# One pool for the tiles of products in a two-layer cross-attention kernel, the order of two weight loads, and the last visit's scaling

## The chip, the cores and the metric

The kernel runs on one core of a Trainium2 chip. Its engines are named as the profile names them: PE (TensorE; its weight loads are the row PEld), DVE (VectorE), ACT (ScalarE), POOL (GpSimd) and SP (SyncE, which here only issues DMAs). The metric is the device time of one execution in microseconds (us), as a median of several runs.

## The reference

Two cross-attention layers with 20 heads of 32 are applied to x (8 batches, 100 rows, 640 channels). Each context has 722 tokens of 1024 channels: 77 of text and 645 of "ip" tokens. Cut to what matters:

```python
q = split(x @ Wq);  k, v = split(text @ Wk), split(text @ Wv)
k_ip, v_ip = split(ip @ Wk_ip), split(ip @ Wv_ip)
out = attend(q, k, v) + attend(q, k_ip, v_ip)       # layer 1
x = merge(out) @ Wo + bo + x

# layer 2: the same with its own weights, and the ip part as
sem = (softmax(q @ k_text.T * scale) @ text) @ ip.T * scale
ip_probs = softmax(q_h @ k_ip.T * scale + 0.5 * sem) * spatial_mask
x = merge(attend(q, k, v) + ip_probs @ v_ip) @ Wout + bout + x
```

Everything is in fp32. The ip tokens' K and V products, 8 x 645 tokens by 1024 by 640 channels for each of four weight matrices, are most of the arithmetic.

## The kernel before, in words

The kernel has a first stage and a main stage.

**First stage (lines 257 to 473).** Inside a nested stack of pools it computes q of layer 1 and, for both layers, k and v of the text tokens and v of the few ip tokens left over after five blocks of 128. Its SBUF tiles come from a pool called "first", which is closed when the stage ends. The text products use a seven-product scheme (`seven`, L187): two-by-two blocked matrices multiplied with seven block products and some additions, where ACT copies a product out of PSUM into the result tile and DVE adds others to it. The result tiles `kt` (L341) and `vt` (L382) have the tag "evs" with two buffers in "first". When a block is finished, POOL issues DMAs that write it to DRAM (L356, L394).

**Main stage.** After "first" and its PSUM pool are closed, new pools are opened (L475 to L484): PSUM pools `ps_sc` for scores (two tags of two banks each, one buffer) and `ps_pt` (two buffers of one bank, for transposes, values and small products), and SBUF pools, the first of which is `opool`, called "made", with two buffers. Tiles in it are the results of the seven-product scheme for the ip tokens: `ko` (L674) for K, `vo` (L644) for V. Where a new pool lies on space that a closed pool held, the first user of a new tile waits for the users of the old ones.

For the first pair of batches and the first two blocks of tokens the task list begins (L714 to L722) with loads: `load_w4` (L550) loads the quarters of the K weights' fifth chunk of 128 channels, two into the tile `wk4` and two into tiles of the pools "tail" and "one"; `load_wv` loads the four quarters of V's ip weights. Then come seven K products (`psk`), the sums of V's weight quarters on DVE (`weight_sums`, L131), seven more K products, the fifth chunk's weight sums and its seven products, and then the V products (`psv`).

**Order.** PE, DVE and ACT run in the order in which the code records the instructions (L44, `manual_schedule`); what SP and POOL issue is placed by a scheduler.

**Visits.** Attention runs over `ORDER`, a list of (unit, chunk): 16 units (a layer and a batch) by 5 chunks of four heads, 80 visits. A visit computes scores in two parts (`scores`, L980), the softmax on DVE and ACT, and then the scaling of the exponentials: `factors` (small operations on DVE, the last L1041), `scaled` (ACT, four instructions of 100x512 at L1047), and `scaled_rest` (DVE, L1055 for the ip tokens after the first 512 and L1051 for text). These are put in the list `later` and recorded at later points. The next visit does `transposes` (L1076): six groups of four PE transposes, each group into a bank of `ps_pt` and copied from there by ACT or DVE (L1088, L1090), and `values` (L1092): 24 products, copied by DVE (L1110). In the last five visits the products' tasks run out. After the last visit the code at L1354 to L1360 records the rest: `last_out` (L950) for the previous visit's values, the six transposes with `at_end=True`, an addition to the residual and its store, `values`, the last `last_out`, its addition and store.

Of the kernel before, what the change touches and what calls it, by code (L numbers as in the profile page):

```python
# [9 lines left out]
F32 = mybir.dt.float32  # L10
AF = mybir.ActivationFunctionType
ALU = mybir.AluOpType
AX = mybir.AxisListType

P = 128
B = 8
S = 100
C = 640
# [5 lines left out]
KA = 512  # L24
# [9 lines left out]
HC = C // 2  # L34
# [6 lines left out]
ORDER = [(u, c) for u in range(NU - 2) for c in range(NC_)]  # L41
# [5 lines left out]
def two_layer_xattn(  # L47
# [17 lines left out]
    nc = tc.nc  # L65
# [3 lines left out]
    wpool = ctx.enter_context(tc.tile_pool(name="w", bufs=1))  # L69
    cpool = ctx.enter_context(tc.tile_pool(name="ctx", bufs=2))  # L70
    spool = ctx.enter_context(tc.tile_pool(name="sums", bufs=1))
    dram = ctx.enter_context(tc.tile_pool(name="scratch", bufs=1, space=bass.MemoryType.DRAM))


# [182 lines left out]
    with ExitStack() as es:  # L257
        fp = es.enter_context(tc.tile_pool(name="first", bufs=1))
# [29 lines left out]
        nc.sync.dma_start(mask_sb[:, 1:2], mask)  # L288


        zeros = fp.tile([P, 2 * S], F32, tag="zeros", name="zeros")
        nc.vector.memset(zeros, 0.0)
        ps = product_ps("zeros_ps")
        for _ in range(4):
# [34 lines left out]
        def text_k(l):  # L329
            t = fp.tile([P, 2, 512], F32, tag="ev", name=f"kt4_{l}", bufs=2)  # L330
            for h in range(2):
                ps = product_ps(f"pskt4_{l}_{h}")
                for k in range(NCC):
                    nc.tensor.matmul(
                        ps[:, :TH], lhsT=W["k", 4][:, k, :], rhs=text[:, k, TH * h : TH * (h + 1)],
                        start=(k == 0), stop=(k == NCC - 1),
                    )
                nc.scalar.copy(t[:, h, :TH], ps[:, :TH])
            nc.gpsimd.dma_start(kt_d[l][4].rearrange("p (h n) -> p h n", h=2), t[:, :, :TH])
            for r in range(2):  # L340
                t = fp.tile([P, 2, 2, C // 2], F32, tag="evs", name=f"kt_{l}_{r}", bufs=2)  # L341

                def product(ps, which, go_on, r=r):
                    for k in range(HK):
                        nc.tensor.matmul(
                            ps[:, :TH], lhsT=W["k", WHICH[which]][:, k, r * P : (r + 1) * P],
                            rhs=sums[which][:, k, :],
                            start=(k == 0 and not go_on), stop=(k == HK - 1), skip_group_check=True,
                        )

                for f in seven(
                    f"pskt_{l}_{r}", product, tuple(t[:, h, m, :TH] for h in range(2) for m in range(2))
                ):
                    f()
                for m in range(2):
                    nc.gpsimd.dma_start(  # L356
                        kt_d[l][2 * m + r].rearrange("p (h n) -> p h n", h=2), t[:, :, m, :TH]
                    )
# [20 lines left out]

        def text_v_blocks(l):  # L380
            for r in range(2):
                t = fp.tile([P, 2, 2, HC], F32, tag="evs", name=f"vt_{l}_{r}", bufs=2)  # L382

                def product(ps, which, go_on, r=r):
                    for k in range(HK):
                        nc.tensor.matmul(
                            ps[:, :HC], lhsT=sums[which][:, k, r * P : (r + 1) * P], rhs=W["v", WHICH[which]][:, k, :],
                            start=(k == 0 and not go_on), stop=(k == HK - 1), skip_group_check=True,
                        )

                for f in seven(f"psvt_{l}_{r}", product, tuple(t[:, h, m] for h in range(2) for m in range(2))):
                    f()
                for h in range(2):
                    nc.gpsimd.dma_start(  # L394
                        vt_d[l][h * TH + r * P : h * TH + (r + 1) * P, :].rearrange("r (m n) -> r m n", m=2), t[:, h]
                    )
# [78 lines left out]
    ps_sc = ctx.enter_context(tc.tile_pool(name="ps_sc", bufs=1, space=PSUM))  # L475
    ps_pt = ctx.enter_context(tc.tile_pool(name="ps_pt", bufs=2, space=PSUM))
    pj[0] = ps_pj
    opool = ctx.enter_context(tc.tile_pool(name="made", bufs=2))
    kpool = ctx.enter_context(tc.tile_pool(name="k", bufs=2))
    vpool = ctx.enter_context(tc.tile_pool(name="v", bufs=2))  # L480
    tpool = ctx.enter_context(tc.tile_pool(name="tail", bufs=2))
# [91 lines left out]
    def pair_tasks(us):  # L573
# [15 lines left out]
        for js in ((0, 1), (2, 3), (4,)):  # L589
# [113 lines left out]
            def with_sums(j, steps, fourth_sum=fourth_sum):  # L703

                return (
                    steps[:1] + [(0.0, lambda: third_sum(j))] + steps[1:4] + [(0.0, lambda: fourth_sum(j))] + steps[4:]
                )
# [6 lines left out]
            if first:  # L714

                v_load = (0.0, lambda: load_wv(wvi[0]))
                v_sums = (0.0, lambda: ([f() for f in weight_sums("v", HC)], load_text(us)))
                v = v_steps(0)
                ks_ = ks_[7:] + [(0.0, w4_sums)] + ks_[:7]
                tasks += [(0.0, load_w4), v_load] + with_sums(0, with_sums(1, ks_[:7]))  # L720
                tasks += [v_sums] + ks_[7:]
                tasks += v[:2] + [(0.0, text_sum)] + v[2:] + v_steps(1)  # L722
            else:

                if js[0]:
                    tasks[ahead:ahead] = head(js[0])
                else:
                    first_sums[us] = head(0)
                for j in js:
                    v = with_sums(j, v_steps(j))  # L730
                    if len(js) == 2 and j == js[0]:
                        v[-2:-2] = head(js[1])
                    tasks += v
                    marks[f"v {j}"] = len(tasks)
                    if j == NB - 1 and us[0] + 2 < B:
                        tasks.append((0.0, lambda: load_text([u + 2 for u in us])))
                tasks += ks_
# [242 lines left out]
    def scores(u, c, part):  # L980
# [31 lines left out]
        def exponentials(h):  # L1012
            for i in (2 * h, 2 * h + 1):
                dst = p[:, i, k0 : k0 + n]
                nc.scalar.activation(  # L1015
                    dst, dst if l else scs[h][:S, i % 2, :n], AF.Exp, bias=st[:, part, i : i + 1],
                    scale=-1.0 if l else 1.0, accum_out=st[:, 3 + part, i : i + 1],
                )
# [13 lines left out]
        def text_exponentials():  # L1032
            nc.scalar.activation(f, f, AF.Exp)
            nc.scalar.activation(p[:, :, NI:], p[:, :, NI:], AF.Exp)

        def factors():
            nc.vector.tensor_reduce(st[:, 5, :], p[:, :, NI:], AX.X, ALU.add)
            nc.vector.tensor_tensor(st[:, 3:5, :], st[:, 3:5, :], f, ALU.mult)
            nc.vector.tensor_tensor(st[:, 4, :], st[:, 3, :], st[:, 4, :], ALU.add)
            nc.vector.reciprocal(rz, st[:, 4:6, :])  # L1040
            nc.vector.scalar_tensor_tensor(  # L1041
                mul, f, mask_sb[:, l : l + 1], rz[:, 0:1, :].to_broadcast([S, 2, 4]), ALU.mult, ALU.mult
            )
# [5 lines left out]
        def scaled_rest(text):  # L1049
            if text:  # L1050
                nc.vector.tensor_tensor(  # L1051
                    p[:, :, NI:], p[:, :, NI:], rz[:, 1, :].unsqueeze(2).to_broadcast([S, 4, NT]), ALU.mult
                )
            else:
                nc.vector.tensor_tensor(  # L1055
                    p[:, :, KA:NI], p[:, :, KA:NI], mul[:, 1, :].unsqueeze(2).to_broadcast([S, 4, NI - KA]),
                    ALU.mult,
                )
# [3 lines left out]
        if part == 0:  # L1062
            later.append((True, lambda: exponentials(0)))
            later.append((True, lambda: exponentials(1)))
        else:
            for h in range(2):
                text_maxima(h)
            differences()
            later.append((True, lambda: (exponentials(0), exponentials(1), text_exponentials())))
            later.append((False, lambda: (factors(), scaled_rest(False))))  # L1070
            later.append((False, lambda: (scaled((0, 1)), scaled_rest(True))))
            later.append((False, lambda: scaled((2, 3))))
# [3 lines left out]
    def transposes(u, c, j, at_end=False):  # L1076
        if j == 0:
            emit(len(later))
            pts[u, c] = one.tile([P, 6, 4 * S], F32, tag="pt", name=f"pt_{u}_{c}")
        rows = P if j < 5 else NTAIL  # L1080
        ps = ps_pt.tile([P, 512], F32, tag="pt", name=f"pspt_{u}_{c}_{j}")
        for i in range(4):
            nc.tensor.transpose(  # L1083
                ps[:rows, i * S : (i + 1) * S], pr[u, c][:, i, j * P : j * P + rows], ident[:S, :S]
            )
        dst, src = pts[u, c][:rows, j, :], ps[:rows, : 4 * S]
        if j in (2, 4) or at_end and j == 0:
            nc.scalar.copy(dst, src)  # L1088
        else:
            nc.vector.tensor_copy(dst, src)  # L1090
# [316 lines left out]
```

## Time and profile before

| What | us |
|---|---|
| Median of 3 runs (2051.62 to 2052.35) | 2052.03 |
| The profiled execution's own time | 2052.75 |
| Its span, from the first to the last instruction | 2051.0 |
| PE busy in it | 2027.9 |
| DVE busy | 1129.7 |
| ACT busy | 784.5 |
| POOL busy | 275.1 |

A table of longer stretches shows where PE is not busy:

```profile
0.00:200.00 200.00, 198.50 (x1027) 146.54 (x1028) 53.38 (x70) 20.75 (x49) 21.96 (x42) 1.00 0.61 193
200.00:230.00 30.00, 24.19 (x94) 19.39 (x92) 10.25 (x14) 1.12 (x3) 4.87 (x7) 0.89 0.55 161
230.00:2030.00 1800.00, 1791.23 (x13845) 1393.73 (x13846) 1054.89 (x2928) 752.82 (x2169) 248.28 (x384) 1.00 0.40 116
2030.00:2051.00 21.00, 13.96 (x199) 11.78 (x198) 11.14 (x36) 9.77 (x28) 0.00 (x0) 0.99 0.07 25
```

Its columns are the stretch in us from the span's start, its length, the busy time of PE, PEld, DVE, ACT and POOL with the number of their instructions, the TensorE clock granted as a share of the full one, the mean busy share of the DMA engines, and GB/s. A matmul that waits is not busy; one that runs at a lower clock is, so idle time and lost clock are read from different columns. The first stage ends, and the main stage begins, at about 203 us.

### The profile page before, as it was taken

How to read it: one execution, taken by the hardware profiler on the slowest of the kernel's cores; microseconds unless marked ns; L12 is line 12 of the kernel's file. 1: busy time of each engine (PE TensorE's matmuls, PEld its weight loads, DVE VectorE, ACT ScalarE, POOL GpSimd, SP SyncE). 2: the span in 40 equal slices, each digit the busy share in tenths (PEclk: the TensorE clock that was granted, in tenths of full speed). 3: DMA queues.
4: the chain of work that ended last, by engine and by line, in shares of the span. 5: the costliest groups of instructions: out<-in, count | busy, mean ns of one | idle time of the engine just before them, and what ended most of it. 6: DMA issues, size and time to landing. Idle time of an engine off the chain costs nothing.

```text
span 2051.0 us, 38714 instructions
## 1 busy us (share of the span) xinstructions
PE 2027.9 (99%) x15162; PEld 1571.4 (77%) x15162; DVE 1129.7 (55%) x3046; ACT 784.5 (38%) x2247; POOL 275.1 (13%) x433
## 2 busy tenths in 40 slices
PE   9999899999999999999999999999999999999998
PEld 9676767776876867778678777777777778889876
DVE  2223322245555455554557665655665667778787
ACT  1001000043334243333433344444544455566676
POOL 0101212110120111111111001001010101111110
PEclk9999999999999999999999999999999999999999
DMA  9544222313342434325346354336342536545461
GB/s 341 152 136 149 89 85 83 102 60 97 100 115 72 138 119 112 91 76 152 97 127 168 93 168 119 86 96 188 95 118 80 148 99 169 151 132 154 119 187 54
DMA packets 296484, 252.20 MB, mean 123 GB/s; under 512 B 46638, under 2 KB 265442, under 8 KB 296302
## 3 DMA queue, kind: packets, MB, share of 16 engines
q1 hardware_dynamic: 274254, 181.19, 32.4%
q0 software_dynamic: 21776, 68.44, 9.3%
q8 instruction: 119, 1.95, 0.4%
q14 instruction: 63, 0.52, 0.1%
q10 hardware_dynamic: 272, 0.10, 0.0%
HBM read 180.74 MB, written 68.93 MB: 122 GB/s over the span
## 4 chain that ended last, share of the span: by engine, by line
PE 95%; DVE 3%; ACT 1%; issue 1%; DMA 0%; ACTq 0%; DVEq 0%
PE psv_a L637 9%; PE psv_d L637 8%; PE pspt L1083 8%; PE psk_a L667 8%; PE psk_d L667 8%; PE sc L992 6%; PE pv L1106 4%; PE psv_e L637 4%; PE psk_c L667 4%; PE psv_b L637 4%; PE psv_c L637 4%; PE psk_e L667 4%; PE psk_b L667 4%; PE pso L904 3%; PE psq L304 2%; PE psq L923 2%
## 5 line engine op out<-in xcount | busy, mean ns | idle before, releaser
L1015 ACT ACTIVATE p<-sc,st 100x512 f32<-100x512 f32 (+1 forms) x320 | 165.6, 529 | 201.9 <-DVE st L1001 120.4
L1047 ACT ACTIVATE p<-p,st 100x512 f32<-100x512 f32 x320 | 208.0, 713 | 51.3 <-DVE st L1041 51.1
L1083 PEld LDWEIGHTS pspt<-ident,p 100*128 100x128 f32 (+1 forms) x1920 | 187.1, 137 | 44.3 <-issue 5.5
L1090 DVE COPY pt<-pspt 128x400 f32<-128x400 f32 (+1 forms) x319 | 175.4, 569 | 81.7 <-PE pspt L1083 73.3
L1083 PE MATMUL pspt<-ident,p 100*128 100x100 f32 (+1 forms) x1920 | 210.0, 250 | 7.3 <-DVE pt L1090 2.1
L1015 ACT ACTIVATE p<-p,st 100x512 f32<-100x512 f32 (+1 forms) x320 | 176.6, 554 | 77.9 <-DVE st L1007 77.8
L637 PE MATMUL psv_a<-wv,x 128*128 128x397 f32 (+1 forms) x560 | 185.8, 474 | 0.6 <-DVE ko L227 0.3
L1088 ACT COPY pt<-pspt 128x400 f32<-128x400 f32 x161 | 79.1, 491 | 264.0 <-PE pspt L1083 263.5
L637 PE MATMUL psv_d<-wv,s 128*128 128x320 f32 (+1 forms) x560 | 174.4, 454 | 0.0
L691 POOL DMA_DIRECT2D k_d<-ko x140 | 100.3, 720 | 460.8 <-DVE ko L227 407.3
L637 PEld LDWEIGHTS psv_a<-wv,x 128*128 128x128 f32 x560 | 103.0, 189 | 68.7 <-issue 13.3
L1007 DVE CUSTOM_DVE_ANT_0 p<-sc,sem 100x512 f32<-100x512 f32 (+1 forms) x320 | 138.7, 490 | 21.8 <-PE sc L992 20.9
L637 PEld LDWEIGHTS psv_d<-wv,s 128*128 128x128 f32 x560 | 103.6, 190 | 52.0 <-issue 2.5
L667 PE MATMUL psk_a<-x,wk 128*128 128x256 f32 (+1 forms) x672 | 137.1, 349 | 4.6 <-ACT ko L201 4.6
L1001 DVE TENSOR_REDUCE st<-sc 100x2 f32<-100x1024 f32 (+1 forms) x160 | 125.3, 825 | 28.7 <-PE sc L992 28.7
L992 PE MATMUL sc<-k,q 32*100 32x210 f32 (+1 forms) x1280 | 138.5, 502 | 0.0
L667 PE MATMUL psk_d<-s,wk 128*128 128x256 f32 (+1 forms) x672 | 136.6, 348 | 0.0
L667 PEld LDWEIGHTS psk_a<-x,wk 128*128 128x128 f32 x672 | 110.5, 190 | 22.9 <-ACT ko L201 5.0
L667 PEld LDWEIGHTS psk_d<-s,wk 128*128 128x128 f32 x672 | 108.5, 189 | 20.4 <-issue 6.7
L652 POOL DMA_DIRECT2D v_d<-vo x70 | 38.9, 556 | 624.6 <-DVE gst L627 318.6
L637 PE MATMUL psv_e<-wvt,x 128*128 128x397 f32 (+1 forms) x280 | 92.9, 474 | 0.0
L1106 PEld LDWEIGHTS pv<-pt,v 128*32 128x32 f32 x3200 | 67.5, 110 | 26.1 <-issue 16.3
(217 smaller groups left out, 3305.4 us busy)
## 6 DMA issues: line engine op xcount, KB each, us to landing
x<-ip_t SPq DMA_DIRECT2D x80, 512.0 KB
k<-k_d SPq DMA_DIRECT2D x80, 322.5 KB
v<-v_d SPq DMA_DIRECT2D x80, 320.0 KB
v_d<-vo POOLq DMA_DIRECT2D x70, 320.0 KB, 2.5
k_d<-ko POOLq DMA_DIRECT2D x112, 128.0 KB, 4.1
o<-wo SPq DMA_DIRECT2D x35, 320.0 KB
x<-ip_t SPq DMA_DIRECT2D x20, 532.0 KB
q<-wq SPq DMA_DIRECT2D x20, 320.0 KB
```

Source lines behind the costliest of these rows:

```text
L637: nc.tensor.matmul(ps[:, :m], lhsT=tokens(k)[:, :P], rhs=w[:, k, :], start=(k == 0 and not go_on), stop=(k == HK - 1), skip_group_check=True,)
L667: nc.tensor.matmul(ps[:, i * m : (i + 1) * m], lhsT=w[:, k, :], rhs=tokens(k), start=(i == 0 and k == 0 and not go_on), stop=(k == HK - 1) ...
L691: nc.gpsimd.dma_start(dst[:, :, r], src)
L992: nc.tensor.matmul(scs[i // 2][:S, i % 2, : k1 - k0], lhsT=qs_[u][rows, c, :], rhs=ks[u, c][rows, k0:k1], start=True, stop=True)
L1001: nc.vector.tensor_reduce(st[:, part, 2 * h : 2 * h + 2], scs[h][:S, :, :n], AX.X, ALU.max, negate=True)
L1007: nc.vector.tensor_tensor_reduce(out=p[:, i, k0 : k0 + n], in0=scs[h][:S, i % 2, :n], in1=sems[u][:, k0 : k0 + n], scale=-1.0, scalar=3.0e ...
L1015: nc.scalar.activation(dst, dst if l else scs[h][:S, i % 2, :n], AF.Exp, bias=st[:, part, i : i + 1], scale=-1.0 if l else 1.0, accum_out= ...
L1047: nc.scalar.activation(p[:, i, :KA], p[:, i, :KA], AF.Copy, scale=mul[:, 0, i : i + 1])
L1083: nc.tensor.transpose(ps[:rows, i * S : (i + 1) * S], pr[u, c][:, i, j * P : j * P + rows], ident[:S, :S])
L1088: nc.scalar.copy(dst, src)
L1090: nc.vector.tensor_copy(dst, src)
L1106: nc.tensor.matmul(ps[32 * i : 32 * i + 32, :S], lhsT=lhs, rhs=pt[:rows, j, i * S : (i + 1) * S], start=(j == 0), stop=(j == 5),)
```

## The change

The pool "made" is opened before the first stage, and the text stage's `kt` and `vt` blocks are tiles of it; the tag "evs" in "first" is gone, and a tile of zeros shares the tag of another small tile. `load_w4` and `load_wv` change places in the first pair's list of tasks. In the last visit the scaling is recorded in one piece: ACT scales heads 0 and 1, and a DVE multiplication with a broadcast operand scales heads 2 and 3 of the first 512 tokens, ahead of the two `scaled_rest` operations. The last visit's transposes 2 and 3 go to the PSUM banks of the scores in place of those of `ps_pt`.

```diff
@@ -69,6 +69,7 @@
     cpool = ctx.enter_context(tc.tile_pool(name="ctx", bufs=2))
     spool = ctx.enter_context(tc.tile_pool(name="sums", bufs=1))
+    opool = ctx.enter_context(tc.tile_pool(name="made", bufs=2))
     dram = ctx.enter_context(tc.tile_pool(name="scratch", bufs=1, space=bass.MemoryType.DRAM))
@@ -288,7 +289,7 @@
-        zeros = fp.tile([P, 2 * S], F32, tag="zeros", name="zeros")
+        zeros = fp.tile([P, 2 * S], F32, tag="evl", name="zeros")
@@ -338,7 +339,7 @@
             for r in range(2):
-                t = fp.tile([P, 2, 2, C // 2], F32, tag="evs", name=f"kt_{l}_{r}", bufs=2)
+                t = opool.tile([P, 2, 2, C // 2], F32, tag="made", name=f"kt_{l}_{r}")
@@ -379,7 +380,7 @@
             for r in range(2):
-                t = fp.tile([P, 2, 2, HC], F32, tag="evs", name=f"vt_{l}_{r}", bufs=2)
+                t = opool.tile([P, 2, 2, HC], F32, tag="made", name=f"vt_{l}_{r}")
@@ -475,7 +476,6 @@
     pj[0] = ps_pj
-    opool = ctx.enter_context(tc.tile_pool(name="made", bufs=2))
     kpool = ctx.enter_context(tc.tile_pool(name="k", bufs=2))
@@ -717,7 +717,7 @@
                 ks_ = ks_[7:] + [(0.0, w4_sums)] + ks_[:7]
-                tasks += [(0.0, load_w4), v_load] + with_sums(0, with_sums(1, ks_[:7]))
+                tasks += [v_load, (0.0, load_w4)] + with_sums(0, with_sums(1, ks_[:7]))
@@ -1067,6 +1067,16 @@
             later.append((True, lambda: (exponentials(0), exponentials(1), text_exponentials())))
+            if (u, c) == ORDER[-1]:
+
+                later.append((False, lambda: (
+                    factors(), scaled((0, 1)),
+                    nc.vector.tensor_tensor(
+                        p[:, 2:, :KA], p[:, 2:, :KA], mul[:, 0, 2:].unsqueeze(2).to_broadcast([S, 2, KA]), ALU.mult
+                    ),
+                    scaled_rest(False), scaled_rest(True),
+                )))
+                return
             later.append((False, lambda: (factors(), scaled_rest(False))))
@@ -1078,7 +1088,10 @@
         rows = P if j < 5 else NTAIL
-        ps = ps_pt.tile([P, 512], F32, tag="pt", name=f"pspt_{u}_{c}_{j}")
+        if at_end and j in (2, 3):
+            ps = ps_sc.tile([P, 2, 512], F32, tag=f"sc{j - 2}", name=f"pspt_{u}_{c}_{j}")[:, 0]
+        else:
+            ps = ps_pt.tile([P, 512], F32, tag="pt", name=f"pspt_{u}_{c}_{j}")
         for i in range(4):
```

## The prediction

> **What bounds the kernel now.** I read the page first, then the table by stretches of time, then the list of waits, then the chain of waits in the two places where the table shows TensorE (PE) short of work. The page says that PE is the bound nearly everywhere:
>
> ```profile
> span 2051.0 us, 38714 instructions
> PE 2027.9 (99%) x15162; PEld 1571.4 (77%) x15162; DVE 1129.7 (55%) x3046; ACT 784.5 (38%) x2247; POOL 275.1 (13%) x433
> PE 95%; DVE 3%; ACT 1%; issue 1%; DMA 0%; ACTq 0%; DVEq 0%
> ```
>
> PE is idle for only 2051.0 - 2027.9 = 23.1 us, so a change that adds or removes no matmul can be worth at most about that, plus what a lowered clock costs. Stretches of 10 us show two places with idle PE: 200 to 230 us, where the text stage hands over to the first K products, and the last 15 us. In steps of 2 us the first place looks like this (columns: stretch, its length, busy PE, PEld, DVE, ACT, POOL, granted PE clock, DMA share, GB/s):
>
> ```profile
> 204.00:206.00 2.00, 2.00 (x11) 1.74 (x10) 0.20 (x1) 0.00 (x0) 1.26 (x2) 1.00 0.89 239
> 206.00:208.00 2.00, 1.13 (x6) 0.64 (x4) 0.00 (x0) 0.00 (x0) 0.14 (x1) 1.00 0.97 294
> 208.00:210.00 2.00, 0.00 (x0) 0.00 (x0) 0.00 (x0) 0.00 (x0) 0.00 (x0) 1.00 0.33 129
> 210.00:212.00 2.00, 0.31 (x1) 0.32 (x2) 0.33 (x1) 0.37 (x1) 0.00 (x0) 0.72 0.02 6
> 212.00:214.00 2.00, 2.00 (x6) 1.55 (x6) 0.69 (x2) 0.00 (x0) 0.00 (x0) 0.50 0.94 274
> 214.00:216.00 2.00, 2.00 (x6) 1.64 (x5) 0.00 (x0) 0.37 (x1) 0.00 (x0) 0.50 0.84 218
> 216.00:218.00 2.00, 2.00 (x7) 1.58 (x7) 0.00 (x0) 0.00 (x0) 0.00 (x0) 0.57 0.99 264
> 218.00:220.00 2.00, 2.00 (x11) 1.75 (x10) 1.02 (x2) 0.00 (x0) 0.00 (x0) 1.00 0.73 232
> ```
>
> The reader should see two losses: no PE work from 207.1 to 211.7, and then about 6 us in which PE is "busy" at half clock, with 6 matmuls in 2 us where it later does 11. The list of waits names the first:
>
> ```profile
> ACT ko L201 <- DMA vt_d<-vt: 15.7, 1, 15.7
> PE psk_a L667 <- ACT ko L201: 4.6, 1, 4.6
> ```
>
> and the chain of waits orders it:
>
> ```profile
> 204.73 5.93 DMA vt_d<-vt
> ...
> 211.26 0.38 ACT ko L201
> 211.64 0.04 issue
> 211.69 3.78 PE psk_a L667 x8
> 215.47 2.90 PE psk_c L667 x8
> ```
>
> PE finished the first two of the seven products, but ACT could not empty the first: its target `ko` is the first tile of the pool "made" (L478), laid where the closed pool "first" was. So it waited for all users of that space, the last being the write of `vt` to DRAM, issued at 204.73.
>
> [...] 4.56 us idle, then 0.50. [...] the `vt` writes here land after 3.0 us in the median and 5.93 us for the last one, beside the weight loads. [...]
>
> **Part 1, one pool for made tiles.** The pool is now opened before "first", and the text stage's `kt`/`vt` blocks are its earlier tiles. The first `ko` thus takes over the buffer of the last-but-one `vt` block, with two writes of its own to wait for (issued at 187.26 and 189.67, long landed). The waits in the changed program say the same: the first ACT copy of `ko` holds only two DMA counts and PE's, where 19 semaphores stood before. The second `ko` waits for the writes of 202.34 and 204.73, landed by 210.7; it is wanted some 7 us later.
>
> What goes: undisturbed steps of this product follow each other at 1.73 us (psk_d 218.20, psk_e 219.94, psk_d 221.66, psk_a of the next block 223.40 in the timeline: 5.20 / 3). From the first step at 203.51, seven steps end at 203.51 + 7 x 1.733 = 215.64. The trace has 223.40. The gain is 7.76 us: 4.56 of idle and 3.2 of low clock, which goes with the idle because nothing else idles PE there.
>
> What is late next: DVE takes up v's weight sums (L135 to L138, started at 223.94) about 7.8 us earlier, near 216.2, with the sum for the next product (L206) queued behind. They need v's last quarter, issued by SP at 203.70. The table shows DMA falling to 0.33 and then 0.02 before SP's next issue at 210.93, so the quarter had landed by 211 at the latest: 5 us of margin. The PE wait of 1.4 us for L206 at 230.14 stays as it is, only earlier. The fifth chunk's weights (L560) no longer wait for the last `vt` write, only for older ones, so SP issues them and the q, vt and residual loads behind them at about 204 instead of 210.93. These 2 MB queue behind the weights and are wanted later. After 245 us no PE wait in the list is for a DMA (the largest is 2.0 us in nine pieces, for DVE), and the x loads follow PE's own progress; so the whole rest moves up by 7.76 us.
>
> **Part 2, v's weights ahead.** SP is scheduled, not pinned: in the trace its four `wv` quarters already go out at 190.78 to 203.70, and the two L560 loads at 210.93. In the built order SP's instructions are the same before and after, so the edit itself costs and gives 0; if I overlook something, no more than the two issues of 0.46 us.
>
> **Part 3, the last visit.** The chain of its end:
>
> ```profile
> 2037.44 0.24 DVE st L1041
> 2037.70 0.71 DVE p L1055
> 2038.41 0.39 DVE p L1051
> 2038.80 0.18 DVE hs L1110
> 2038.99 0.04 issue
> 2039.03 1.36 PE pso_last L956 x10
> 2040.39 0.36 PE pspt L1083 x4
> 2040.77 0.50 ACT pt L1088
> ```
>
> Four ACT scalings (L1047, 2.56 us from 2037.76) become two; heads 2 and 3 become one DVE multiplication of 100x1024. The rows of 532 and 308 elements start 0.63 and 0.39 us before their successors, so (0.63 - 0.39) / 224 = 1.07 ns an element; 1024 elements hold DVE for 0.63 + 492 x 0.00107 = 1.16 us. [...] It is queued ahead of L1055, L1051 and L1110, the copy of the previous visit's values that PE's last_out needs, and PE does last_out before the transposes. ACT being done at about 2039.0 instead of 2040.3 is therefore hidden: PE starts last_out at 2039.03 + 1.15 = 2040.18 and the transposes are 1.15 us later.
>
> What comes back: with two more PSUM banks, transposes 2 and 3 need not wait for copies 0 and 1. Counting from the first transpose (2040.22), groups of four are now ready 0.34 us apart, after the 0.55 from its start to the first ACT copy. ACT copies 0, 2, 4 then start at 0.55, 1.23, 1.91 and last 0.50, and the values' matmuls start at 2.45; before they started at 2043.61 - 2040.22 = 3.39. That is 0.94 back. The residual add on DVE (0.67) then begins at about 2.75 and is done by 3.45, before the last values copy at 3.76. Net: 1.15 - 0.94 = 0.2 us later. Bounds: +1.2 if the banks bring nothing, -0.9 if the multiplication were hidden; I take +0.2, as DVE works in order and every row is in the trace.
>
> **Sum.** 2051.0 - 7.76 + 0.2 = 2043.4 us of span. The profiled run took 2052.75, or 1.75 around its span, so 2045.2; it lies 0.72 above the median of 2052.03, which leaves 2044.5 beside that median, 0.37% less. (About 0.2%, 4.1 us, can be told from no change.)
>
> **Rivals.**
> A, as above, 2044.5 with 2043.0 to 2046.5: 0.82.
> B, the idle goes but low clock, or a new short wait of the same size, stays: -4.56 + 0.2, so 2047.7. For it: the clock's cause is not in the trace; against it: 0.998 mean clock, all of whose loss (0.002 x 2051 = 4 us) fits the one dip after the idle. 0.10, a little over half of it beyond 0.2%.
> C, something else still holds the copy, and only the end changes: 2052.2. Against it stand the two remaining counts. 0.04.
> D, slower: v's last quarter comes late, because the loads now issued at 204 compete with it and with the `vt` writes. DVE stands at L135 with L206 behind it, and PE stops at the second psk_c. If the quarter lands at X, L206 is done at X + 6.1 (sums 223.94 to 229.67, then 0.4). Before, PE went on at 230.14 after paying 3.2 of low clock; with a new idle it pays a similar 3.2 again, so it is slower from X of about 224. At X = 229.4, PE goes on at 235.5: +5.4 + 0.2, or 2057.6. Against it: it would take 25 us for what took at most 7. 0.04.
>
> Chances: faster 0.82 + 0.06 = 0.88; same 0.04 (B) + 0.04 (C) = 0.08; slower 0.04. The range 2043.0 to 2047.2 holds A and the near side of B.
>
> **What would show it.** Right: no PE wait for ACT L201's successor; clock 1.00 from 200 to 220 us; the second block's psk_a near 215.6; L560 issued near 204; at the end a DVE multiplication of about 1.24 us, last_out later by about 1.15, and values' matmuls 2.4 us after the first transpose. Wrong: a clock dip that stays, DVE idle at L135 for a load, or a stretch past 245 us in which PE waits for DMA.

## The result, and the profile after

The changed kernel takes 2047.15 us in the median of 11 runs (2045.36 to 2048.51), the kernel before beside it 2051.66 (11 runs, 2050.55 to 2053.12): a ratio of 0.9977, 95% interval 0.9967 to 0.9986, or 4.5 us less. That lies in the range on record, but only 0.05 us inside its upper end of 2047.2: 7.6 us were forecast.

The handover is as predicted. The chain of waits of the changed kernel (start, us, what) has no DMA and no ACT step in it:

```profile
203.75 1.73 PE psk_a L667 x8
205.48 1.73 PE psk_b L667 x8
207.21 1.73 PE psk_a L667 x8
208.94 1.73 PE psk_c L667 x8
...
215.86 1.73 PE psk_a L667 x8
```

Every step takes 1.73 us. In the timeline the second block begins at 215.70, 12.11 us after the first psk_a at 203.59, against 19.89 before. What is late next is what was named: in the list of waits, PE's 1.4 us for DVE's `ko` behind the weight sums (now L207), unchanged, and after it no wait for a DMA. SP issues L560 at 204.51; DVE takes up the weight sums at 216.24 without waiting for a load. The same list has a new first row:

```profile
PE pso_last L956 <- DVE hs L1123: 3.0, 2, 2.6
PE pspt L1096 <- DVE pt L1103: 2.1, 8, 0.6
```

The longest of its two waits was 1.4 us before. What follows it shows in the table by stretches at the end (stretch, length, busy PE, PEld, DVE, ACT, POOL, PE clock, DMA share, GB/s):

```profile
2030.00:2032.00 2.00, 0.21 (x12) 0.00 (x0) 1.93 (x4) 1.33 (x2) 0.00 (x0) 1.00 0.03 8
2032.00:2033.00 1.00, 0.21 (x1) 0.22 (x2) 0.73 (x3) 0.00 (x0) 0.00 (x0) 0.84 0.00 0
2033.00:2034.00 1.00, 1.00 (x6) 1.00 (x6) 0.00 (x0) 0.00 (x0) 0.00 (x0) 0.50 0.00 0
...
2038.00:2039.00 1.00, 1.00 (x8) 0.90 (x6) 0.52 (x1) 0.39 (x1) 0.00 (x0) 0.50 0.00 0
2039.00:2040.00 1.00, 1.00 (x34) 0.83 (x36) 0.72 (x2) 0.11 (x1) 0.00 (x0) 0.75 0.00 0
```

The dip, the stretch at half clock, that left 212 us is back at 2033, behind the idle before last_out. The chain of waits at the end gives its price:

```profile
2030.06 0.23 DVE st L1041
2030.30 0.02 issue
2030.32 1.23 DVE p L1074
2031.55 0.62 DVE p L1055
2032.17 0.39 DVE p L1051
2032.56 0.18 DVE hs L1123
2032.74 0.04 issue
2032.79 2.46 PE pso_last L956 x10
2035.24 4.00 PE pspt L1096 x24
2039.24 1.36 PE pv L1119 x48
```

Up to L1123 the rows last about as long as predicted (the multiplication 1.23 us for 1.16; the 128x1024 weight sums, L135, take 1.22 in before), and last_out starts 2.73 us after L1041 where it started 1.59 after it before: 1.14 later, for 1.15. But the ten last_out instructions take 2.46 us where they took 1.36 before, and the transposes 4.00 at half speed.

The dip is not in every execution. The spans and mean clocks of the 11 runs (us) fall into groups:

```
clock 1.000   2043.6  2043.7  2043.8  2044.1
clock 0.999   2045.0  2045.4  2045.5
clock 0.998   2046.4  2046.5  2046.6  2046.7
```

The first group stands about where the sum put the span (2043.4); the second is some 1.6 us later, the last some 2.8. A second profile of the changed kernel, from the run after_again, is one of a smaller loss:

```profile
2032.00:2034.00 2.00, 0.22 (x2) 0.22 (x3) 1.73 (x4) 0.71 (x2) 0.00 (x0) 1.00 0.00 0
2034.00:2036.00 2.00, 2.00 (x14) 2.00 (x14) 0.00 (x0) 0.00 (x0) 0.00 (x0) 0.62 0.00 0
2036.00:2038.00 2.00, 2.00 (x15) 2.00 (x14) 0.57 (x1) 0.81 (x2) 0.00 (x0) 0.53 0.00 0
2038.00:2040.00 2.00, 1.76 (x54) 1.55 (x56) 1.69 (x3) 0.67 (x2) 0.00 (x0) 1.00 0.00 0
```

Worked out from the clock column, the clock is low from 2034.5 to 2037.9 here, 3.4 us, and from 2032.7 to 2039.5 in the first profile, 6.8 us.

### The profile page after: what moved, and what is told of

It reads as the page before. It is cut to its first block, busy times and chain, and to the rows that moved or that the text cites. A ratio compares the mean times of both kernels' runs of the same rounds, so it can differ in the third digit from the quotient of the medians.

```text
span 2046.5 us, 38708 instructions
## 1 busy us (share of the span) xinstructions
PE 2027.1 (99%) x15162; PEld 1573.3 (77%) x15162; DVE 1130.6 (55%) x3047; ACT 783.0 (38%) x2245; POOL 274.1 (13%) x433
## 4 chain that ended last, share of the span: by engine, by line
PE 95%; DVE 4%; ACT 1%; issue 0%; DMA 0%; SPq 0%; DVEq 0%
PE psv_a L637 9%; PE psv_d L637 8%; PE pspt L1096 8%; PE psk_a L667 8%; PE psk_d L667 7%; PE sc L992 6%; PE pv L1119 4%; PE psv_e L637 4%; PE psk_b L667 4%; PE psk_c L667 4%; PE psv_b L637 4%; PE psv_c L637 4%; PE psk_e L667 4%; PE pso L904 3%; PE psq L923 2%; PE psq L305 2%
```

## The experiments

Theory G: the new DVE multiplication lengthens PE's idle before last_out enough for the clock to fall in some executions, which takes back up to 3 us. It has two rivals: R1, that the handover is worth less than the profile says, and R2, that the spread of 3 us has nothing to do with the end. The last column of the table is from one profiled execution of each: the us from the last L1041's start to the start of the last addition, L964, in the chain of waits. The rows were measured on several chips, each with the kernel before beside it, so kernels are compared by their ratios and traces before their medians. The ratio lies near the quotient of the means, which for p3_end are 2.4 us apart where the medians are 3.2.

| Kernel | Runs | Median us | Lowest to highest | Before beside it | Ratio (95%) | L1041 to last L964 |
|---|---|---|---|---|---|---|
| before | | | | | | 9.26 |
| changed | 11 | 2047.15 | 2045.36 to 2048.51 | 2051.66 | 0.9977 (0.9967 to 0.9986) | 12.35 |
| p1_pool | 6 | 2045.76 | 2045.19 to 2046.59 | 2051.80 | 0.9969 (0.9958 to 0.9981) | 9.26 |
| p3_end | 13 | 2055.03 | 2051.58 to 2056.86 | 2051.80 | 1.0011 (1.0003 to 1.0019) | 12.24 |
| e_banks | 5 | 2044.59 | 2043.96 to 2045.19 | 2051.80 | 0.9964 (0.9950 to 0.9977) | 8.34 |
| e_fill | 5 | 2045.64 | 2044.94 to 2046.01 | 2051.80 | 0.9968 (0.9955 to 0.9980) | 9.48 |
| e_order | 5 | 2043.61 | 2043.01 to 2043.80 | 2052.12 | 0.9958 (0.9946 to 0.9971) | 7.30 |
| e_dose | 21 | 2049.74 | 2048.60 to 2050.99 | 2052.12 | 0.9989 (0.9983 to 0.9996) | 13.43 |
| e_handfill | 21 | 2049.86 | 2048.89 to 2051.13 | 2052.12 | 0.9989 (0.9983 to 0.9996) | 9.26 |
| p2_swap | 12 | 2051.46 | 2051.13 to 2052.74 | 2052.12 | 0.9999 (0.9991 to 1.0007) | 9.25 |
| e_order_act | 5 | 2044.94 | 2044.23 to 2045.45 | 2052.56 | 0.9963 (0.9949 to 0.9976) | 8.29 |
| after_again | 9 | 2047.60 | 2046.13 to 2048.60 | 2052.56 | 0.9975 (0.9966 to 0.9985) | 11.12 |

**p1_pool, part 1 alone.** The four edits of the pool, nothing else:

```diff
+    opool = ctx.enter_context(tc.tile_pool(name="made", bufs=2))
...
-                t = fp.tile([P, 2, 2, HC], F32, tag="evs", name=f"vt_{l}_{r}", bufs=2)
+                t = opool.tile([P, 2, 2, HC], F32, tag="made", name=f"vt_{l}_{r}")
```

> Part 1 alone: the made pool opened first, the end as before. Theory G (the longer idle of TensorE at the end lets its clock fall in some executions): the handover's 7.7 us are gained whole in the profile, the clock is 1.00 throughout, span about 2043.3, and the single runs lie within about 1 us of each other; ratio to before about 0.9965. Rival R1 (the handover gives only some 4.5 us in the median): ratio about 0.9978. Rival R2 (the spread of 3 us is noise that has nothing to do with the end): runs spread over 3 us here too.

Six runs lie within 1.4 us, five of them at clock 1.000. The sixth, 0.999, is the profiled one, and its clock falls only at 2041.48, after the last product has ended: the mean clock counts such a fall too, though it costs nothing. From the first psk_a to the second block's it is 12.11 us, as in the changed kernel; the end is that of before, 9.26. Against R2, the spread of 3.2 us is not there with the old end, though six runs are few. Of R1 something stays: the median gain is 6.0 us, not 7.7. And some spread has nothing to do with either place: the first psk_a starts between 203.13 us (e_banks) and 204.78 (p1_pool) in the profiles.

**p3_end, part 3 alone.**

```diff
+            if (u, c) == ORDER[-1]:
+                later.append((False, lambda: (factors(), scaled((0, 1)),
+                    nc.vector.tensor_tensor(p[:, 2:, :KA], ..., ALU.mult),
+                    scaled_rest(False), scaled_rest(True))))
+                return
...
+        if at_end and j in (2, 3):
+            ps = ps_sc.tile([P, 2, 512], F32, tag=f"sc{j - 2}", ...)[:, 0]
```

> Part 3 alone (the last visit's DVE multiplication, one piece of scaling, two more PSUM banks), the handover as before. Theory G: slower than before by 0.2 us in executions in which the clock holds at the end and by up to 3.3 us where it falls, 1 to 3 us in the median: ratio 1.0005 to 1.0015. R1 and R2: 0.2 us, ratio 1.0001.

Slower than before, by 3.2 us in the median, a little more than Theory G's 1 to 3. Three of 13 runs have clock 0.999 and spans of 2049.8 to 2050.0, which is the level of before; nine have 0.997 and 2052.2 to 2053.8, one 0.995 and 2055.1. The profiled one is of the nine, and its chain of waits shows the end's cost again:

```profile
2039.78 0.18 DVE hs L1123
2039.96 0.04 issue
2040.01 2.46 PE pso_last L956 x10
2042.46 4.00 PE pspt L1096 x24
```

**e_banks, the changed kernel without the DVE multiplication.** ACT scales four heads as before; the two more PSUM banks stay (the block with `ORDER[-1]` above is taken out).

> The changed kernel with the last visit's scaling as before (four ACT scalings, no DVE multiplication), but with the two more PSUM banks for its transposes. Theory G: last_out starts 1.15 us earlier than in the changed kernel, TensorE idles for 1.4 us as before, the clock holds; the values' matmuls follow the first transpose after 2.4 us instead of 3.4; span about 2042.4, ratio about 0.996, runs within about 1 us. R1: some 2046 to 2047. R2: the spread stays at 3 us.

```profile
2031.12 0.04 issue
2031.17 1.36 PE pso_last L956 x10
2032.53 1.73 PE pspt L1086 x20
2034.26 0.02 issue
2034.28 0.50 ACT pt L1091
2034.79 0.04 issue
2034.83 1.28 PE pv L1109 x48
```

This is the chain of waits of that kernel: last_out at full clock, the transposes in one run of 1.73 us, and the end 9.26 - 8.34 = 0.92 us shorter than before. The prediction had worked out 0.94 for the banks.

**e_fill, idle filled with work.** The changed kernel with

```diff
+        warm = ps_sc.tile([P, 2, 512], F32, tag="sc1", name="warm")
+        for _ in range(8):
+            nc.tensor.matmul(warm[:, 0, :P], lhsT=ident, rhs=ident, start=True, stop=True)
         last_out(0, [NC_ - 1])
```

> The changed kernel with eight 128x128x128 fp32 matmuls more on TensorE between the previous visit's values and last_out, which write a PSUM bank that nothing reads: they fill the idle of 2.6 us and delay nothing if they take less. Theory G: the clock stays at 1.00 to the end in every execution, span 2043.5 to 2043.9, runs within about 0.7 us: more work and faster than the changed kernel by about 2 us in the median. R1 and R2: the same time and spread as the changed kernel, or slower.

Eight matmuls whose result nothing reads, and the kernel is 1.5 us faster than the changed one in the medians, with a spread of 1.1 in place of 3.2. The intervals of the two ratios overlap; the timeline of PE shows what happens:

```profile
2030.09 0.36 PE L1119 MATMUL pv<-pt,vt 82*32 82x100 f32 x8
2030.38 2.05 PE L1369 MATMUL warm<-ident 128*128 128x128 f32 x16
2033.02 1.36 PE L956 MATMUL pso_last<-hs,wol 128*128 128x100 f32 x10 [0.59 <-DVE hs L1123]
```

The wait that is left is 0.59 us, last_out is at full clock, and the end takes 9.48 us: 0.22 more than before, which is the +0.2 of the prediction. What the changed kernel loses beyond it in its profile, 12.35 - 9.48 = 2.87 us, is clock.

**e_dose, idle lengthened.** The changed kernel with the multiplication first done once more, into the previous visit's tile:

```diff
+                    nc.vector.tensor_tensor(
+                        pr[ORDER[-2]][:, 2:, :KA], p[:, 2:, :KA], mul[:, 0, 2:]..., ALU.mult
+                    ),
```

> The changed kernel with the last visit's DVE multiplication done twice (the first time into a tile that nothing reads any more). TensorE's idle before last_out grows from 2.6 to about 3.7 us. Theory G: the clock falls in every or nearly every execution; time 1.2 us above the slowest of the changed kernel's runs, about 2049.5, ratio about 0.999, hardly any run with a clock of 1.00. R1 and R2: 1.2 us above the changed kernel's median, about 2048.3, with the same spread.

The idle grows to 3.8 us in the list of waits, and not one of 21 runs has a clock of 1.000 (19 have 0.998, one 0.999, one 0.996). Their times say the same: the shortest span, 2046.8 us, is 2.7 above the longest of the changed kernel at clock 1.000 (2044.1), where the second multiplication accounts for 1.2. With 1.4 us of idle the clock held until the last product in the profiles of p1_pool and e_banks; with 2.6 it falls in some executions; with 3.8 in all.

**e_order, the copy ahead of the multiplication.** The last visit's `factors` are recorded, then the previous visit's values, then the scaling:

```diff
-            emit(len(later))
+            emit(len(later) - (n == len(ORDER) - 1))
             if last:
                 values(*last)
...
-                later.append((False, lambda: (
-                    factors(), scaled((0, 1)),
+                later.append((False, factors))
+                later.append((False, lambda: (
+                    scaled((0, 1)),
```

> The changed kernel with one thing moved: the last visit's factors are recorded, then the previous visit's values and their copy, and then the scaling. DVE copies the values before its multiplication, so last_out starts some 2.2 us earlier than in the changed kernel and lies beside the multiplication. Theory G: TensorE's longest idle at the end falls under 1 us, the clock holds, the transposes start when the multiplication ends, about 1 us before the place they have in the kernel with one pool alone; span about 2041.5, ratio about 0.9955, the fastest so far, runs within about 1 us. R1 and R2: 1 to 2 us under the changed kernel with the same spread of 3 us.

The chain of waits:

```profile
2030.48 0.23 DVE st L1041
2030.71 0.27 DVE hs L1124
2030.98 0.04 issue
2031.03 1.36 PE pso_last L956 x10
2032.38 1.73 PE pspt L1097 x20
```

The copy comes right after L1041, last_out runs beside the multiplication, and the transposes start 1.90 us after L1041 (before 2.95, changed 5.18). The longest wait for the copy is 0.4 us. With 2043.61 us against 2052.12 it has the lowest ratio of all, 0.9958, and its five runs lie within 0.8 us.

**e_order_act, the same without the multiplication.** `scaled((0, 1, 2, 3))`, and the DVE instruction left away.

> As the kernel with the values' copy moved ahead, but all four heads scaled by ACT and no DVE multiplication. Theory G: last_out starts early and the clock holds, but the transposes wait for ACT's fourth scaling, so the time is that of the kernel with the banks alone, about 1 us above the kernel with the copy moved and the multiplication, ratio about 0.9963. Rival: the multiplication brings nothing and both are equal, ratio 0.9958.

Here the end takes 8.29 us, as with the banks alone (8.34): in the chain ACT's four scalings stand before the transposes with 2.57 us. So the multiplication is worth 8.29 - 7.30 = 1.0 us where the copy doesn't stand behind it. The two ratios, 0.9963 and 0.9958, can't be told apart by their intervals; the traces, one of each kernel, do it.

**e_handfill, the low clock of the handover by itself.** The kernel before, with 14 matmuls in the wait between the second and third product:

```diff
                     made[0][i]()
+                    if i == 1 and us[0] == 0 and js[0] == 0 and rs == [0]:
+                        warm = ps_sc.tile([P, 2, 512], F32, tag="sc1", name="warm")
+                        for _ in range(14):
+                            nc.tensor.matmul(warm[:, 0, :P], lhsT=ident, rhs=ident, start=True, stop=True)
```

> The kernel before with fourteen 128x128x128 fp32 matmuls more (3.6 us) on TensorE between the second and third product of the first K block, into a bank that nothing reads: they fill the idle of the handover without ending the wait. Theory G and the prediction's sum: the idle's 4.6 us stay, the low clock after it goes, 2 to 3.2 us faster than before, ratio about 0.9987. If the low clock has another cause: the same as before, ratio 1.000.

2.3 us less than before in the medians with the wait for the DMA still there. The table by stretches shows clock 1.00 throughout:

```profile
208.00:210.00 2.00, 1.95 (x18) 1.76 (x16) 0.00 (x0) 0.00 (x0) 0.00 (x0) 1.00 0.12 48
210.00:212.00 2.00, 0.88 (x4) 0.81 (x5) 0.90 (x2) 0.37 (x1) 0.00 (x0) 1.00 0.12 29
212.00:214.00 2.00, 2.00 (x11) 1.75 (x10) 0.12 (x1) 0.37 (x1) 0.00 (x0) 1.00 1.11 300
```

So of the 6.0 us of p1_pool some 2.3 are clock and, by difference, the other 3.7 idle.

**p2_swap, part 2 alone.**

```diff
-                tasks += [(0.0, load_w4), v_load] + with_sums(0, with_sums(1, ks_[:7]))
+                tasks += [v_load, (0.0, load_w4)] + with_sums(0, with_sums(1, ks_[:7]))
```

> Part 2 alone: the two load tasks change places. All theories: nothing, ratio 1.000, since SP issues the loads in the same order; the spread of its runs is that of the kernel before.

Nothing, 0.9999. It gives another execution of the old handover, and a cheaper one. The timeline:

```profile
203.95 1.89 PE L667 MATMUL psk_a<-x,wk 128*128 128x256 f32 x8
205.68 1.89 PE L667 MATMUL psk_b<-s,wkt 128*128 128x256 f32 x8
211.29 3.11 PE L667 MATMUL psk_a<-x,wk 128*128 128x256 f32 x8 [3.72 <-ACT ko L201]
...
221.73 1.89 PE L667 MATMUL psk_a<-x,wk 128*128 128x256 f32 x8
```

Here the idle is 3.72 us and the first psk_a to the second block's 17.78 us, where the profile of before had 4.56 and 19.89, and p3_end's 4.69 and 19.41. The low clock is shorter as well: 3.4 us by the clock column (0.83 over 210 to 220), from about 212.0 to 215.4 as an estimate from the two longer steps, where it lasted 6.8 in before (210.88 to 217.71) and in p3_end (0.66 over 210 to 220).

**after_again, the changed kernel beside other experiments.**

> The changed kernel once more, beside the others on one chip: runs spread from about 2045.4 to 2048.5, those at clock 1.00 under 2046.2 and those at 0.998 above 2048; ratio about 0.9975.

One run of nine has clock 1.000 (2046.13 us), the others 0.999 and 2047.04 to 2048.60. The ratio is that of the first measurement; the group of 0.998 that was expected did not come. The profile, whose clock column stands in the section on the result, has the same idle of 2.6 us before last_out, a low clock half as long, and an end of 11.12 us in place of 12.35. Beside e_fill's 9.48 the fall costs 1.6 us here and 2.9 in the first profile, which fits the distances between the groups of runs. Neither the share of runs with a dip nor its length is fixed.

## Why the prediction was right and where it was off

- *Part 1, the wait goes and nothing takes its place*: right. Step by step the handover runs as laid out; the second block's psk_a was predicted at 215.6 and came at 215.70, SP's loads at 204.51, and DVE did not wait for v's last quarter.
- *Part 1, its size, "The gain is 7.76 us"*: the term was too large. It was read from one execution in which both the landing of the `vt` write (5.93 us) and the dip (6.8 us) were long; in p2_swap's profile they are about 5.1 (an estimate: 5.93 less the 4.56 - 3.72 = 0.84 us by which PE idles shorter) and 3.4. Over three profiles the old handover costs 19.89, 19.41 and 17.78 us against 12.11, or 5.7 to 7.8; p1_pool's medians say 6.0. "3.2 of low clock, which goes with the idle" was an estimate from that one execution (4.56 us idle, then a clock of 0.50); it is right in kind (e_handfill, 1.00 with the idle filled), about 2.3 in size.
- *Part 2, 0*: right (p2_swap).
- *Part 3, "Net: 1.15 - 0.94 = 0.2 us later"*: right for an execution at full clock (e_fill 0.22, and the banks by themselves -0.92 in e_banks), and still the step that failed for the kernel as it stands. It counted the 1.15 us by which last_out starts later as time only, and not as PE's longer idle: 2.57 us in place of 1.44. Its reason, "nothing else idles PE there", was true of the handover; the change itself made the next such place. The clock falls there in some executions, for up to 3 us. The medians of the changed kernel and p1_pool, 2047.15 and 2045.76, differ by 1.4 us where 0.2 was forecast.
- Together: of the 3.1 us that are missing from the 7.6, part 1's size takes some 1.7 and the end 1.4 - 0.2 = 1.2. This is no independent check, since the 1.4 is itself a difference of the medians; part 3 alone costs more, 3.2 in the median, with 10 of 13 runs in its slower groups against 7 of 11 of the changed kernel.
- That the total still came to lie in the range is luck. Path A, whose mechanism part 1 followed, had 2043.0 to 2046.5, and 2047.15 is outside it, in the part that was added for rival B.
- Rival B gave the measured size, "low clock, or a new short wait of the same size, stays". The low clock did not stay at the handover; it came up at the other end. C and D did not come: no count held the copy, and v's last quarter had landed in time.
- How much idle lowers the clock, and for how long: an unbroken idle of 2.57 us was enough in the profiled execution of the changed kernel and of p3_end. A low clock that ends while PE works lasts 3.4 us (p2_swap, after_again) or 6.8 (before, changed, p3_end, e_dose). The same 2.6 us of idle are not followed alike: in the changed kernel's profile the fall comes 0.11 us before last_out starts, in after_again's some 0.7 us after. What sets the place of the fall and which of the two lengths it has is not shown: no run set either on purpose. That length of idle and fall go together is shown by e_fill (0.59 us left, last_out at 1.36) and e_dose (3.8 us, no run of 21 at 1.000).

## What to carry to other kernels

An instruction put on an engine costs its own time and whatever stands behind it in that engine's order (here 1.23 us on DVE, and last_out 1.14 later); where TensorE waits for that, price the wait twice, as time and as idle that may lower the clock (another 2.87 us in the changed kernel's profile). A small copy that feeds TensorE belongs ahead of a long elementwise operation (e_order: an end of 7.30 us for 12.35). And a stall read from one profile is one draw (the old handover: 19.89, 19.41 and 17.78 us): look at a second execution before its length goes into a sum.

## What the runs showed that had not been expected

TensorE idle of 1.4 us left the clock alone in the profiles of p1_pool and e_banks, 2.6 us lowered it in some executions, 3.8 in all 21. But 1.4 us is no safe length: in p1_pool's profile the clock fell 1.07 us after the end of the last product, where nothing was left to slow. The fall lasts 6.8 us at 0.50 in the changed kernel's profile and costs 2.9 us, more than the 1.1 us by which the idle grew; in after_again's it lasts 3.4 and costs 1.6. Eight matmuls of 0.26 us each, done for nothing, gave back 1.5 us in the medians.
